# Turning the second sequence's first norm on VectorE and by transfers, with one feature order for both sequences and the mask made earlier

## The chip, the core and the metric

One core of one Trainium2 chip runs the whole program. Its engines, as the profile names them, are PE (TensorE: matmuls and transposes, with PEld for the loading of its weights), DVE (VectorE), ACT (ScalarE), POOL (GpSimd) and SP (SyncE, which issues most of the transfers). They run beside each other and wait for each other at semaphores. The metric is the device time of one execution in microseconds (us), as a median over runs. All arithmetic is in 32-bit floats.

## The reference

Two sequences of 512 tokens with 256 features go through four sublayers, each of the form `x = x + layernorm(f(layernorm(x)))`:

```python
x = x + _layernorm(_L0_attn_ref(_layernorm(x), ...))   # 16 heads of 128, causal
x = x + _layernorm(_L0_ffn_ref(_layernorm(x), ...))    # 4-bit weights, 2048 hidden
x = x + _layernorm(_L1_attn_ref(_layernorm(x), ...))   # linear attention
x = x + _layernorm(_L1_ffn_ref(_layernorm(x), ...))    # 16-entry table, 688 hidden
```

The change lies in the first line. The attention begins with a second norm, which has a gain and an offset for each feature, and then makes q, k and v:

```python
x = (h - mu) * rsqrt(var + EPS) * ln_g + ln_b
q = (x @ wq.T + bq); k = (x @ wk.T + bk); v = (x @ wv.T + bv)
q, k = rope(q), rope(k)
attn = softmax(where(causal, -inf, q @ k.T * scale))
```

## The kernel before, in words

**Tiles.** A sequence is four tiles of 128 tokens (`NT`), a token's 256 features are two chunks of 128 (`NK`). The norm is made with tokens on the partitions (tile `n`), but the projections contract over the features, so the normed values must be turned: `xT0[b]` holds, for sequence b, the features on the partitions and the 512 tokens along them. `xTv[b]` is a copy of it with the tokens in another order, for v. For both sequences, PE turned the tiles before (`turn`, L622, which calls `transpose`, L277), into a PSUM bank; `affine` (L625) then applied gain and offset on the way from the bank to `xT0`.

**first_norms (L564)** does this. It is a generator: at each `yield` it hands back the time until it wants to go on. For sequence 0 (`wait` is 0, L646 on) it works as fast as it can, because nothing else can start before: tiles 0 and 1 are centred by ACT (L657) and turned and scaled by a matmul with a diagonal; tiles 2 and 3 are centred by DVE (`centred`, L611) and turned by PE. For sequence 1 (L631 on) it makes one tile's statistics at a time (`statistics`, `variance`, `factor`, `finished`) and then, chunk by chunk, four transposes into a bank and one `affine`. At the end both copy `xT0` to `xTv` (L696), and later make the residual for their attention (L705 on).

**Later norms** (`norms`, L342) turn in the other way already: DVE transposes the tile in blocks of 32 by 32 into `tr` (L375), and four transfers (L379) bring the blocks to their partitions. The features then lie in another order along the partitions, and the weights that are contracted with them are laid out to fit on the host (`turned`, L1395). `chunk` (L319) reads such a tile in runs of 32.

**The order of the work.** Heads of both sequences are 32 slots (`slot`, L1021). In slot i, PE makes the scores of head i, the projections of head i+1, the output projection of head i-2, the attention of head i-1 and a part of v. DVE adds the mask and finds the minima (`scores`), ACT takes exponentials, DVE, ACT and POOL apply the rotation to q and k (`projection`, L802). POOL adds the two parts of k as its last step in a slot, and the scores of the next slot need this k. Only for head 0 does DVE add k (L846). Beside this, the 4-bit weights are dequantised in steps put off by `behind`, and the table weights are built by `look_up`, a DVE and a POOL instruction a step.

The order is fixed when the program is built. A planner adds up assumed costs (`Engine.cost`, L109) into a clock `now`, and `poll` (L250) lets every chain go on by a step whose due time has come. In a slot, `poll` is called twice near the end (L1112 and L1119), with a part of v between. `begin(first_norms(1, 6.0), 60.0)` (L1142) gives sequence 1's norm its start, 60 planned us after the first head's preparation, and 6 planned us between steps. Each engine's instructions, and SP's transfers, then run in the order in which they were written.

**The mask** is a tile of 128 by 512: cleared by POOL at the start (L560), and its causal part is filled by one `affine_select` on POOL (L1130). That stood after the two projections of head 0, and ahead of the first v and of head 1's q.

Of the kernel before, what the change touches and what calls it, by code (L numbers as in the profile page):

```python
# [10 lines left out]
F32 = mybir.dt.float32  # L11
# [8 lines left out]
P = 128  # L20
B = 2
# [167 lines left out]
def sandwich_kernel(  # L189
# [309 lines left out]
    with ExitStack() as at:  # L499
# [49 lines left out]


        xTv = [ac.tile([P, NK, S], F32, name=f"xTv_{b}") for b in range(B)]
        xT0 = [ac.tile([P, NK, S], F32, name=f"xT0_{b}") for b in range(B)]
        acc = ac.tile([P, NT, D], F32, name="h")


# [8 lines left out]
        def first_norms(b, wait):  # L564

            n = [
                acts.tile([P, HT, D], F32, tag="ln", name=f"n0_{b}_{j}") for j in range(NT // HT)  # L570
            ]
            st = small.tile([P, NT, 6], F32, tag="st0", name="st0", bufs=2)
            mv = small.tile([P, NT, 2], F32, tag="mv0", name="mv0", bufs=2)
            ve = small.tile([P, 2, NT], F32, tag="ve0", name="ve0", bufs=2)
            rstd = small.tile([P, 2, NT], F32, tag="rstd0", name="rstd0", bufs=2)
            shift = small.tile([P, 2, NT], F32, tag="shift0", name="shift0", bufs=2)

            def factors(k, ts, scale, more):
                vector.tensor_scalar(
                    ve[:, k, ts], mv[:, ts, 1], scale, more, ALU.mult, ALU.add  # L580
                )
                pool.tensor_tensor(rstd[:, k, ts], ve[:, k, ts], mhalf[:, ts], ALU.pow)

            def shifted(k, ts):
                vector.scalar_tensor_tensor(
                    shift[:, k, ts], mv[:, ts, 0], -1.0, rstd[:, k, ts], ALU.mult, ALU.mult
                )

            def norm(k, t, to):
                scalar.activation(  # L590
                    to,
                    x0[b][:, t, :],
                    AF.Identity,
                    bias=shift[:, k, t : t + 1],
                    scale=rstd[:, k, t : t + 1],
                )

            def finished(t):
                shifted(0, slice(t, t + 1))
                norm(0, t, n[t // HT][:, t % HT, :])  # L600

            def statistics(t):
                vector.bn_stats(st[:, t, :], x0[b][:, t, :])

            def variance(t):
                vector.bn_aggr(mv[:, t, :], st[:, t, :])

            def factor(t):
                factors(0, slice(t, t + 1), 1.0 + EPS, EPS * EPS)

            def centred(t):  # L611

                vector.tensor_scalar(
                    n[t // HT][:, t % HT, :],
                    x0[b][:, t, :],
                    mv[:, t, 0:1],
                    rstd[:, 0, t : t + 1],
                    ALU.subtract,
                    ALU.mult,
                )  # L620

            def turn(pt, kc, t):  # L622
                transpose(pt, n[t // HT][:, t % HT, kc * P : (kc + 1) * P])

            def affine(engine, to, pt, kc):  # L625
                if engine is scalar:
                    scalar.activation(to, pt, AF.Identity, bias=col("b", kc), scale=col("g", kc))
                else:
                    vector.tensor_scalar(to, pt, col("g", kc), col("b", kc), ALU.mult, ALU.add)

            if wait:  # L631
                for t in range(NT):
                    statistics(t)
                    variance(t)
                    factor(t)
                    if t:
                        finished(t - 1)
                    yield wait
                finished(NT - 1)
                yield 2 * wait  # L640
                for kc in range(NK):
                    pt = bank("t")
                    for t in range(NT):
                        turn(pt[:, t * P : (t + 1) * P], kc, t)
                    affine(scalar, xT0[b][:, kc, :], pt, kc)
                    yield wait  # L646
            else:

                minus = wu[:, 0, :P]
                scalar.mul(minus, ident, -1.0)
                for t in range(NT):
                    statistics(t)
                    variance(t)
                    if t < HT:
                        scalar.activation(  # L657
                            n[0][:, t, :], x0[b][:, t, :], AF.Identity, bias=mv[:, t, 0:1], scale=-1.0
                        )
                    factor(t)  # L660
                    if t < HT:
                        scalar.activation(
                            wu[:, 0, (t + 1) * P : (t + 2) * P],
                            minus,
                            AF.Identity,
                            scale=rstd[:, 0, t : t + 1],
                        )

                quarters = [[bank(tag) for _ in range(NK)] for tag in "ts"]
                for t in range(HT):  # L670
                    for kc in range(NK):
                        matmul(
                            quarters[0][kc][:, t * P : (t + 1) * P],
                            n[0][:, t, kc * P : (kc + 1) * P],
                            wu[:, 0, (t + 1) * P : (t + 2) * P],
                            True,
                            True,
                        )
                    if t == 0:
                        warm_up(2)  # L680
                centred(2)
                centred(3)
                for j in range(2):
                    if j:
                        yield 0.0
                        for kc in range(NK):
                            for t in (HT, HT + 1):
                                turn(quarters[1][kc][:, t % HT * P : (t % HT + 1) * P], kc, t)
                    for kc in range(NK):
                        affine(  # L690
                            scalar,
                            xT0[b][:, kc, j * TU : (j + 1) * TU],
                            quarters[j][kc][:, :TU],
                            kc,
                        )
            for kc in range(NK):  # L696
                (scalar.copy if kc or wait else pool.tensor_copy)(
                    xTv[b][:, kc, :].rearrange("p (t a j) -> p t j a", t=NT, j=4),
                    xT0[b][:, kc, :].rearrange("p (t j a) -> p t j a", t=NT, j=4),
                )  # L700
            yield 30.0
            while holder[0] is not None:
                yield 4.0
            holder[0] = b
            every = slice(0, NT)  # L705
            factors(1, every, 1.0, EPS)
            yield 2.0
            shifted(1, every)
            yield 2.0
            for t in range(NT):  # L710
                norm(1, t, acc[:, t, :])
                pool.tensor_add(acc[:, t, :], acc[:, t, :], bo_sb)
                yield 3.0

        first = first_norms(0, 0.0)
        next(first)

        def dequantised(packed, scales, u, name, w):

# [82 lines left out]
        def projection(kind, i, tag="mm"):  # L802
# [10 lines left out]
            for cs in [slice(0, TU), slice(TU, S)] if i == 0 else [slice(0, S)]:  # L813
                ps = bank(tag)
                for kc in range(NK):
                    matmul(
                        ps[:, cs],
                        w[:, hh, kc, :],
                        xT0[b][:, kc, cs],
                        kc == 0,  # L820
                        kc == NK - 1,
                    )
# [304 lines left out]
        next(pair[1])  # L1127
        for step in (*pair, *pair):
            next(step, None)
        pool.affine_select(  # L1130
            out=mask,
            in_=mask,
            compare_op=ALU.is_ge,
            fill=NEG,
            base=S - P,
            pattern=[[-1, S]],
            channel_multiplier=1,
        )
        values(0, 0, "t")
        project("q", 1, "o")  # L1140

        begin(first_norms(1, 6.0), 60.0)  # L1142
        main = ffn_hidden(0)
        for i in range(NS + 2):
            slot(i)
# [227 lines left out]
def _layout(i):  # L1373
# [4 lines left out]
    a0, f0, a1, f1 = "L0_attn_", "L0_ffn_", "L1_attn_", "L1_ffn_"  # L1378

    def by_group(w):  # L1380
        return w.reshape(NG, HG * DK, NK, P).transpose(0, 3, 2, 1)

    def by_head_chunk(w):
        return w.reshape(NG, HG, DK, NK, P).transpose(0, 4, 1, 3, 2)

    def by_head(v):
        return v.reshape(-1, P).T
# [10 lines left out]
    def by_half(s):  # L1398
# [16 lines left out]
        "wk": by_head_chunk(i[a0 + "wk"]),  # L1415
        "wv": by_group(i[a0 + "wv"]),
        "wo": i[a0 + "wo"].reshape(D, NG, HG, DK).transpose(1, 3, 2, 0),
        "cols": np.concatenate([by_head(i[a0 + n]) for n in ("bq", "bk", "bv", "ln_g", "ln_b")], axis=1),
        "bo": i[a0 + "bo"][None, :],
        "cos": np.concatenate([cos, cos]),  # L1420

# [33 lines left out]
```

## Time and profile before

| what | us |
|---|---|
| median of 3 runs | 628.33 |
| lowest and highest run | 627.58, 628.52 |
| the profiled execution's own time | 627.55 |
| its span, first to last instruction | 625.8 |
| PE busy in it | 618.7 |
| DVE busy | 486.7 |
| ACT busy | 299.4 |
| POOL busy | 277.6 |

The profile comes from one execution, and durations taken from it add up to its span, not to the median of the runs. A row of the timeline gives start and duration; several like instructions that follow each other are one row with a count. Matmuls overlap in PE, so that the distance from start to start, not the duration, says what one costs. Slots can be recognised by the rows `ps_s<-kT,qT` on PE: slot 0 starts at 15.16, slot 5 at 65.69 and slot 10 at 121.71. The last scores of the 32 slots are masked at about 362 us; what follows is mostly the three other sublayers.

### The profile page before, as it was taken

To read this page: it belongs to the slowest core of one execution; us is meant where nothing else is said; L and a number is where in the kernel's file an instruction comes from. 1 tells how busy PE (TensorE), PEld (TensorE's weight loads), DVE (VectorE), ACT (ScalarE), POOL (GpSimd) and SP (SyncE) were. 2 spreads that over 40 slices of the span, in tenths; PEclk is the share of its full clock that TensorE was granted. 3 is DMA by queue.
4 is the path that set the end of the run, shared out by engine and by line. 5 is a ranking of instruction groups with operands and counts; after the bars stand their busy time and mean duration, and the time that the engine had idled before them with its cause. 6 is when DMAs were issued, how large, how long until landed. Compare 5 with 4: busy or idle time off the path is not lost.

```text
span 625.8 us, 8236 instructions
## 1 busy us (share of the span) xinstructions
PE 618.7 (99%) x2512; PEld 462.7 (74%) x2512; DVE 486.7 (78%) x1155; ACT 299.4 (48%) x659; POOL 277.6 (44%) x350
## 2 busy tenths in 40 slices
PE   8999999999999999999999999999999999999996
PEld 6666666666666666666666778888888888888886
DVE  6879789877887989999988988869986373284853
ACT  5656666656655556656556661232313404416130
POOL 5264657455454375675667400350261151163341
PEclk9999999999999999999999999999999999999999
DMA  7467374564656646556453422211001001001000
GB/s 252 108 158 213 96 201 128 125 174 123 139 158 143 170 126 167 153 133 181 119 139 77 89 57 62 101 35 34 1 5 30 1 1 35 0 1 34 26 26 18
DMA packets 43004, 60.07 MB, mean 96 GB/s; under 512 B 5072, under 2 KB 30928, under 8 KB 42960
## 3 DMA queue, kind: packets, MB, share of 16 engines
q1 hardware_dynamic: 42672, 59.39, 36.5%
q8 instruction: 20, 0.33, 0.2%
q14 instruction: 24, 0.20, 0.1%
q10 hardware_dynamic: 288, 0.16, 0.1%
HBM read 28.33 MB, written 1.05 MB: 47 GB/s over the span
## 4 chain that ended last, share of the span: by engine, by line
PE 97%; DMA 1%; POOL 1%; ACT 0%; issue 0%; DVE 0%; SPq 0%; POOLq 0%
PE ps_mm L272 39%; PE ps_s L272 22%; PE ps_o L272 21%; PE ps_t L272 14%; DMA x<-in_x 0%; DMA cos_sb<-in_cos 0%; ACT xT L181 0%; PE ps_t L278 0%; POOL qT L181 0%; ACT xTv L181 0%; POOL ra L181 0%; DVE kT L181 0%; SPq L163 0%; POOLq L1451 0%; POOL rstd L181 0%
## 5 line engine op out<-in xcount | busy, mean ns | idle before, releaser
L181 DVE SCALAR_TENSOR_TENSOR rr<-ps_mm,cols_sb,sin_sb 64x512 f32<-64x512 f32 (+1 forms) x126 | 93.4, 741 | 3.8 <-PE ps_mm L272 1.0
L181 POOL TENSOR_TENSOR wg<-wg,scratch 128x752 f32<-128x752 f32 x30 | 53.6, 1787 | 92.0 <-DVE scratch L181 89.2
L272 PE MATMUL ps_mm<-xT,wg 128*128 128x256 f32 (+1 forms) x352 | 84.9, 379 | 0.0
L181 ACT ACTIVATE p<-p,mn 128x512 f32<-128x512 f32 (+3 forms) x128 | 70.6, 553 | 29.4 <-DVE mn L181 29.4
L272 PE MATMUL ps_s<-xT,wu 128*128 128x256 f32 x336 | 81.0, 379 | 0.0
L272 PE MATMUL ps_o<-wd,hT 128*128 128x256 f32 (+1 forms) x364 | 78.2, 372 | 0.0
L272 PE MATMUL ps_t<-pT,v 128*128 128x512 f32 (+3 forms) x256 | 74.2, 433 | 0.0
L272 PEld LDWEIGHTS ps_o<-wd,hT 128*128 128x128 f32 x364 | 67.4, 190 | 8.8
L272 PEld LDWEIGHTS ps_mm<-xT,wg 128*128 128x128 f32 (+1 forms) x352 | 66.4, 189 | 9.3 <-ACT ge L181 0.3
L272 PEld LDWEIGHTS ps_s<-xT,wu 128*128 128x128 f32 x336 | 63.8, 190 | 8.8
L272 PEld LDWEIGHTS ps_t<-pT,v 128*128 128x128 f32 x256 | 48.6, 190 | 27.9 <-issue 16.3
L181 DVE CUSTOM_DVE_ANT_0 p<-ps_s,mask 128x512 f32<-128x512 f32 (+2 forms) x96 | 45.8, 509 | 28.4 <-PE ps_s L272 28.2
L181 ACT ACTIVATE p<-p,rs 128x512 f32<-128x512 f32 (+3 forms) x128 | 61.4, 550 | 10.7 <-DVE rs L181 8.8
L272 PEld LDWEIGHTS ps_o<-wo,oT 128*128 128x128 f32 x256 | 48.6, 190 | 19.0 <-issue 12.9
L181 POOL TENSOR_TENSOR qT<-ra,rr 128x512 f32<-128x512 f32 x32 | 40.8, 1276 | 48.8 <-DVE rr L181 48.8
L272 PE MATMUL ps_s<-kT,qT 128*128 128x512 f32 (+2 forms) x192 | 60.8, 452 | 0.2 <-DVE kT L181 0.2
L272 PE MATMUL ps_o<-wo,oT 128*128 128x256 f32 x256 | 60.5, 379 | 0.0
L272 PE MATMUL ps_mm<-xT,wq 128*128 128x512 f32 (+1 forms) x128 | 58.6, 580 | 0.4 <-ACT xT L181 0.4
L272 PE MATMUL ps_mm<-xT,wk 128*128 128x512 f32 x124 | 58.3, 592 | 0.0
L272 PEld LDWEIGHTS ps_s<-kT,qT 128*128 128x128 f32 x192 | 36.0, 190 | 26.9 <-issue 15.0
L181 DVE STREAM_TRANSPOSE turned<-p 128x512 f32<-128x512 f32 (+3 forms) x128 | 54.1, 480 | 1.6 <-ACT p L181 0.7
L272 PE MATMUL ps_mm<-wv,xTv 128*128 128x256 f32 x232 | 54.9, 379 | 0.0
(146 smaller groups left out, 914.9 us busy)
## 6 DMA issues: line engine op xcount, KB each, us to landing
pT<-turned SPq DMA_DIRECT2D x128, 208.0 KB, 3.9
wo<-in_wo SPq DMA_DIRECT2D x17, 256.0 KB, 4.0
wv<-in_wv SPq DMA_DIRECT2D x16, 256.0 KB, 4.1
wq<-in_wq SPq DMA_DIRECT2D x15, 256.0 KB, 4.0
wk<-in_wk SPq DMA_DIRECT2D x15, 256.0 KB, 4.0
xT<-tr SPq DMA_DIRECT2D x44, 64.0 KB, 2.2
pk_g<-in_gate_p SPq DMA_DIRECT2D x4, 256.0 KB, 5.2
sc_g<-in_gate_s SPq DMA_DIRECT2D x8, 128.0 KB, 4.7
```

Of the source, the lines that this page charges most:

```text
L181: return write(*args, **more)
L272: nc.tensor.matmul(out, lhsT=lhsT, rhs=rhs, start=start, stop=stop, **more)
```

## The change

- The turning of sequence 1 leaves PE. Its four tiles are transposed by DVE in blocks of 32 by 32 into a part of `wd` (a tile that is filled later), and four transfers of 32 partitions each bring the blocks into `xT0[1]`, which gets the shape of a turned tile. `affine` then works on `xT0[1]` in place, from SBUF to SBUF, and the projections of sequence 1 read it through `chunk`.
- The feature order that results holds for both sequences, since they share the weights. For sequence 0, the two statements that write `n` (the DVE one in `centred` and the ACT one) read their tile through a view (`spread`), so that PE's transposes come out in this order; reading goes in steps of 32 floats, writing is in a row.
- The weights and the two columns for gain and offset are laid out to fit on the host.
- The mask's select is issued on POOL right after the first part of sequence 0's norm, ahead of the projections.
- Sequence 1's norm is due after 45 planned us instead of 60, with waits of 1 instead of 6.

The diff:

```diff
--- before.py
+++ after.py
@@ -549,7 +549,11 @@
 
 
         xTv = [ac.tile([P, NK, S], F32, name=f"xTv_{b}") for b in range(B)]
-        xT0 = [ac.tile([P, NK, S], F32, name=f"xT0_{b}") for b in range(B)]
+
+
+        xT0 = [
+            ac.tile([P, NK, S] if b == 0 else [P, 4, NK, NT, 32], F32, name=f"xT0_{b}") for b in range(B)
+        ]
         acc = ac.tile([P, NT, D], F32, name="h")
 
 
@@ -608,11 +612,19 @@
             def factor(t):
                 factors(0, slice(t, t + 1), 1.0 + EPS, EPS * EPS)
 
+            def spread(t):
+
+                return (
+                    n[t // HT][:, t % HT, :].rearrange("p (k f c) -> p k f c", k=NK, c=4),
+                    x0[b][:, t, :].rearrange("p (k c f) -> p k f c", k=NK, c=4),
+                )
+
             def centred(t):
 
+                to, x = spread(t)
                 vector.tensor_scalar(
-                    n[t // HT][:, t % HT, :],
-                    x0[b][:, t, :],
+                    to,
+                    x,
                     mv[:, t, 0:1],
                     rstd[:, 0, t : t + 1],
                     ALU.subtract,
@@ -637,12 +649,26 @@
                         finished(t - 1)
                     yield wait
                 finished(NT - 1)
-                yield 2 * wait
+                yield until(*n)
+
+                tr = wd.rearrange("p o d -> p (o d)")[:, : NK * S].rearrange(
+                    "p (c k j t) -> p c k j t", c=4, k=NK, j=NT
+                )
+                for t in range(NT):
+                    vector.transpose(
+                        tr[:, :, :, t, :],
+                        n[t // HT][:, t % HT, :].rearrange("p (k c f) -> p c k f", k=NK, c=4),
+                    )
+                    yield wait
+                for a in range(4):
+                    sync.dma_start(
+                        out=xT0[b][:, a].rearrange("p k j t -> p (k j t)"),
+                        in_=tr[32 * a : 32 * a + 32].rearrange("f c k j t -> f c (k j t)"),
+                    )
+                yield until(xT0[b])
                 for kc in range(NK):
-                    pt = bank("t")
-                    for t in range(NT):
-                        turn(pt[:, t * P : (t + 1) * P], kc, t)
-                    affine(scalar, xT0[b][:, kc, :], pt, kc)
+                    x = xT0[b][:, :, kc].rearrange("p a j t -> p a (j t)")
+                    affine(scalar, x, x, kc)
                     yield wait
             else:
 
@@ -655,7 +681,7 @@
                     variance(t)
                     if t < HT:
                         scalar.activation(
-                            n[0][:, t, :], x0[b][:, t, :], AF.Identity, bias=mv[:, t, 0:1], scale=-1.0
+                            *spread(t), AF.Identity, bias=mv[:, t, 0:1], scale=-1.0
                         )
                     factor(t)
                     if t < HT:
@@ -696,7 +722,9 @@
             for kc in range(NK):
                 (scalar.copy if kc or wait else pool.tensor_copy)(
                     xTv[b][:, kc, :].rearrange("p (t a j) -> p t j a", t=NT, j=4),
-                    xT0[b][:, kc, :].rearrange("p (t j a) -> p t j a", t=NT, j=4),
+                    xT0[b][:, kc, :].rearrange("p (t j a) -> p t j a", t=NT, j=4)
+                    if b == 0
+                    else xT0[b][:, :, kc].rearrange("p j t a -> p t j a"),
                 )
             yield 30.0
             while holder[0] is not None:
@@ -714,6 +742,15 @@
 
         first = first_norms(0, 0.0)
         next(first)
+        pool.affine_select(
+            out=mask,
+            in_=mask,
+            compare_op=ALU.is_ge,
+            fill=NEG,
+            base=S - P,
+            pattern=[[-1, S]],
+            channel_multiplier=1,
+        )
 
         def dequantised(packed, scales, u, name, w):
 
@@ -816,7 +853,7 @@
                     matmul(
                         ps[:, cs],
                         w[:, hh, kc, :],
-                        xT0[b][:, kc, cs],
+                        chunk(xT0[b], kc) if b else xT0[b][:, kc, cs],
                         kc == 0,
                         kc == NK - 1,
                     )
@@ -1127,19 +1164,10 @@
         next(pair[1])
         for step in (*pair, *pair):
             next(step, None)
-        pool.affine_select(
-            out=mask,
-            in_=mask,
-            compare_op=ALU.is_ge,
-            fill=NEG,
-            base=S - P,
-            pattern=[[-1, S]],
-            channel_multiplier=1,
-        )
         values(0, 0, "t")
         project("q", 1, "o")
 
-        begin(first_norms(1, 6.0), 60.0)
+        begin(first_norms(1, 1.0), 45.0)
         main = ffn_hidden(0)
         for i in range(NS + 2):
             slot(i)
@@ -1378,10 +1406,10 @@
     a0, f0, a1, f1 = "L0_attn_", "L0_ffn_", "L1_attn_", "L1_ffn_"
 
     def by_group(w):
-        return w.reshape(NG, HG * DK, NK, P).transpose(0, 3, 2, 1)
+        return w.reshape(NG, HG * DK, NK, 4, 32).transpose(0, 4, 3, 2, 1).reshape(NG, P, NK, HG * DK)
 
     def by_head_chunk(w):
-        return w.reshape(NG, HG, DK, NK, P).transpose(0, 4, 1, 3, 2)
+        return w.reshape(NG, HG, DK, NK, 4, 32).transpose(0, 5, 4, 1, 3, 2).reshape(NG, P, HG, NK, DK)
 
     def by_head(v):
         return v.reshape(-1, P).T
@@ -1415,7 +1443,11 @@
         "wk": by_head_chunk(i[a0 + "wk"]),
         "wv": by_group(i[a0 + "wv"]),
         "wo": i[a0 + "wo"].reshape(D, NG, HG, DK).transpose(1, 3, 2, 0),
-        "cols": np.concatenate([by_head(i[a0 + n]) for n in ("bq", "bk", "bv", "ln_g", "ln_b")], axis=1),
+        "cols": np.concatenate(
+            [by_head(i[a0 + n]) for n in ("bq", "bk", "bv")]
+            + [turned(by_head(i[a0 + n])) for n in ("ln_g", "ln_b")],
+            axis=1,
+        ),
         "bo": i[a0 + "bo"][None, :],
         "cos": np.concatenate([cos, cos]),
```

## The prediction

> **What bounds the kernel now.** I read four views: the head of the page, what TensorE (PE) waited for, the timeline where the changed lines run, and the timeline of the first 23 us. The columns of a timeline are start, duration (us), engine, line, operation, tiles, shapes, count and the idle time before.
>
> ```profile
> span 625.8 us, 8236 instructions
> PE 618.7 (99%) x2512; PEld 462.7 (74%) x2512; DVE 486.7 (78%) x1155; ACT 299.4 (48%) x659; POOL 277.6 (44%) x350
> PE 97%; DMA 1%; POOL 1%; ACT 0%; issue 0%; DVE 0%; SPq 0%; POOLq 0%
> ```
>
> PE is the chain that ends last. Its waits in the whole execution are four, and all lie in the first 16 us:
>
> ```profile
> PE ps_o L546 <- POOL ident masks.py:199: 1.4, 1, 1.4
> PE ps_mm L272 <- ACT xT L181: 0.4, 1, 0.4
> PE ps_t L272 <- ACT wu L181: 0.3, 1, 0.3
> PE ps_s L272 <- DVE kT L181: 0.2, 1, 0.2
> ```
>
> So time can come from PE work that is removed, or from the start. VectorE (DVE), busy 78%, is next, but nothing in PE waits for it later. The work removed, at its first place, with its neighbours:
>
> ```profile
> 131.18 1.89 PE L272 MATMUL ps_mm<-wv,xTv 128*128 128x256 f32 x8
> ...
> 132.91 0.60 PE L278 MATMUL ps_t<-ident,n 128*128 128x128 f32 x4
> ...
> 133.35 1.89 PE L272 MATMUL ps_s<-kT,qT 128*128 128x512 f32 x6
> ```
>
> Four transposes stand between the starts 132.91 and 133.35, so they cost 0.44 us, not the 0.60 of the row and not four times their 0.272. The slots confirm it: the scores start at 99.30, 110.50 and 121.71 (11.2 us apart) and then at 133.35 and 144.99 (11.64 apart, in both cases with four transposes inside).
>
> At the start, the mask and what stands around it:
>
> ```profile
> 12.64 1.27 POOL L181 TENSOR_TENSOR qT<-ra,rr 128x512 f32<-128x512 f32 x1
> 13.08 1.88 PE L272 MATMUL ps_o<-xT,wq 128*128 128x512 f32 x4
> ...
> 13.86 0.61 POOL L181 TENSOR_SCALAR_AFFINE_SELECT mask<-mask 128x512 f32<-128x512 f32 x1
> 13.94 1.08 DVE L181 TENSOR_TENSOR kT<-ra,rr 128x512 f32<-128x512 f32 x1
> ...
> 15.16 1.96 PE L272 MATMUL ps_s<-kT,qT 128*128 128x512 f32 x6 [0.20 <-DVE kT L181]
> ...
> 21.72 0.66 DVE L181 TENSOR_TENSOR kT<-ra,rr 128x512 f32<-128x512 f32 x1
> ```
>
> The same addition takes 1.08 us beside the mask's select and 0.66 alone. The first scores wait for its end at 15.02.
>
> [...] The trace has this pair already (tr<-ln at 0.426 us for 128x256; xT<-tr landing in 2.2 us).
>
> **The change, part by part.**
>
> PE work removed: eight transposes in two groups of 0.44 make **-0.88**. Nothing follows them that hides it, as PE waits for nothing there. The projections of the second sequence now read xT0 in runs of 32. I take zero: ps_t<-pT,v reads runs of 32 and has 592 ns for 512 columns, wq from plain xT0 also 592; 256 columns from xT1 in runs have 379, as from plain weights. A gain is excluded, since nothing there is shortened; were each of the 128 matmuls (0.43 us) 1% longer, it would be 0.5, which I keep as the upper bound.
>
> VectorE added: four transposes of 0.426, 1.7 us, over two slots of 11.2 us. ScalarE: the affine reads SBUF, not PSUM; the same size from SBUF is 0.72 (p<-p,rs) against 0.78, so nothing. The two xTv copies (2.04 us together) stay at one place.
>
> The start of the norm moves from 60 to 45 planned us and its waits from 6 to 1. The planner polls twice near the end of a slot, some 1.7 us apart, and before the first statistics ran at 75.9, the end of slot 5 (slot 5 starts at 65.69). Fifteen us earlier is the end of slot 4, and now both polls serve it: tiles 0 and 1 at the end of slot 4, tiles 2 and 3 at the end of slot 5, the last shift in slot 6, transposes in slots 6 to 8, transfers then, affines and copies in slots 9 to 11. xTv is first read at the end of slot 14 and xT0 in slot 15 (from 178.6): over 30 us of cover, and without it every late us would stop PE.
>
> A tile step is 0.79 us on VectorE (75.91 to 76.70), 0.87 with a shift. Slot 4 gains 1.7 us: VectorE waited 2.43 us at 66.75 for PE, which hides it. Slot 5 has two steps in place of one, +1.0 us: there VectorE is already late, its scores start at 78.35 where PE's are ready at about 77.5. Of the 1.0, 0.45 is taken up by its wait ahead of ra at 81.04. The other 0.55 reaches POOL's last step for the slot:
>
> ```profile
> 83.47 1.28 POOL L181 TENSOR_TENSOR qT<-ra,rr 128x512 f32<-128x512 f32 x1 [1.02 <-DVE rr L181]
> 84.69 1.28 POOL L181 TENSOR_TENSOR ra<-ra,cos_sb 128x512 f32<-128x512 f32 x1
> 86.06 1.28 POOL L181 TENSOR_TENSOR kT<-ra,rr 128x512 f32<-128x512 f32 x1
> ```
>
> kT ends at 87.34 and PE wants it at 88.10, so 0.76 is free and 0.2 is left: **0**, bounds 0 and +0.6. In slots 6 to 9 two transposes (0.85) replace one step (0.87): 0. Each shift now waits, within a slot, for POOL's power (0.55 us, 1.54 [...]); behind it on VectorE stand the dequantised weights' product (1.41) and the next scores, for which ScalarE's exponentials and then kT wait. That is the 0.6.
>
> SyncE (SP): four transfers of 128 KB go into its queue, some 2.9 to 3.3 us of issue as for xT<-tr and pT, behind the pT transfers of that slot and ahead of the next slot's loads. They wait for the four transposes. Behind them stand weights for two slots later, whose loads take 4 us: 0. If that cover were gone, 3 us would be PE's.
>
> The mask: its select goes behind the four powers on POOL, the last of which ends at 7.13, where POOL was idle until 9.37. kT then takes 0.66 and ends at 14.60. Now PE's own queue is late next: 13.08 and four matmuls of 0.43 give 14.80 against 15.16, so **-0.36** at most.
>
> What it meets there: centred(3) on VectorE starts at 7.16, waiting for the same power, and is a tensor_scalar from SBUF. POOL goes first. The earlier centred(2), 0.14 longer (below), holds the fourth power to about 7.27; the select ends near 7.88 [...]; centred(3) ends at about 8.33. Its transpose was due at 8.25 (8.11 and 0.14), so PE is late by about 0.13.
>
> The feature order: both statements write in a row and read in steps of 32. ScalarE has the form at 599.87:
>
> ```profile
> 599.87 0.83 ACT L181 ACTIVATE ln<-x,shift,rstd 128x256 f32<-128x256 f32 x1 [2.05 <-POOL shift L181]
> ```
>
> 0.83 against 0.60 for the plain one: +0.23. The first such instruction ends at 4.74 instead of 4.51, hidden by the wait for the power (wu starts at 4.84). The second delays wu from 5.97 to 6.20, and PE's matmuls, which followed the warm-up at 6.18, to about 6.25: +0.07. On VectorE, [...] I take 0.14 (0.41 becomes 0.55)[...]. The 0.07 and 0.13 fall on one path and don't add: **+0.14**, bounds 0.05 and 0.5. It could not be below zero, since nothing there is shortened.
>
> Sum: -0.88 - 0.36 + 0.14 = -1.10. The profiled execution has 627.55 (span 625.8 and 1.75 around it), so 626.45. The median of the runs, 628.33, lies 0.78 above it; with the same step, **627.2**.
>
> **Rivals.** (1) The start gives nothing: select and hops delay PE by the whole 0.36 or by up to 0.3 more. For it: transpose and centred(3) are only 0.1 us apart. Against: PE needs this only once. 627.45 to 627.8. (2) The start gives all, and the earlier scores free VectorE too: 628.33 - 0.88 - 0.36 = 627.1, down to 626.6. [...] (3) Slower: two tile steps a slot put the POOL powers onto VectorE's path. If each waits the 1.54 of the row at 77.30, VectorE is 2.1 us late; 0.45 and 0.76 absorb 1.2, so 0.9 us a slot reaches PE through kT; in four slots 3.6, that is 628.33 - 1.1 + 3.6 = 630.8. It decides from 1.2 us of lateness, and to be slower outright takes 2.4 us in all. Against: in slot 5 the power stands ahead of the product that would block it. (4) The order written out after slot 16 comes out otherwise, because the planner's clock stands 0.9 us lower: either sign, about 1 us.
>
> **Numbers.** Chances: the sum as it stands (626.8 to 627.5) 0.45, rival 1 0.20, rival 2 0.15, rival 3 0.12, rival 4 0.08. 0.2% of 628.33 is 1.26 us, about what this measurement tells from no change; the sum lies just inside. Faster by more: 0.4 of the first case, rival 2 and a third of rival 4, 0.38; slower: rival 3, 0.12; between: 0.50. The range, 626.5 to 628.7, leaves out rival 3 and the edges.
>
> **What would show it.** PE's x8 group from n at 272 ns gone and slots 10 and 11 at 11.2 us; kT's first at 0.66; first scores near 14.94; n<-x,mv near 0.73 on ScalarE and 0.55 on VectorE; no PE wait for kT at slot 7. Wrong would be: slots 4 to 9 longer than 11.2, or projections above 592 ns.

## The result and the profile after

| | before | after |
|---|---|---|
| median of 22 runs each, taken side by side (us) | 628.11 | 626.80 |
| lowest and highest | 627.49, 628.66 | 626.49, 627.73 |
| the profiled execution's own time | 627.55 | 626.75 |
| its span | 625.8 | 625.0 |

The ratio is 0.9983, with a 95% interval from 0.9976 to 0.9989: about 1.1 us faster (0.7 to 1.5), where 1.1 was forecast. The means of the runs lie 1.09 us apart, the medians 1.31. The interval leaves out 1, so it is a gain, though at 0.17% it lies inside the 0.2% that the prediction took as the limit of what can be told from no change.

The head of the page and its chain of work, by engine:

```profile
span 625.0 us, 8231 instructions
PE 618.0 (99%) x2504; PEld 462.0 (74%) x2504; DVE 488.3 (78%) x1159; ACT 299.9 (48%) x659; POOL 276.7 (44%) x350
PE 98%; DMA 0%; issue 0%; DVE 0%; POOL 0%; ACT 0%; POOLq 0%
```

PE has eight instructions less, VectorE four more. What PE's matmuls waited for in the whole execution:

```profile
PE ps_o L546 <- POOL ident masks.py:199: 1.4, 1, 1.4
PE ps_mm L272 <- ACT xT L181: 0.4, 1, 0.4
PE ps_t L272 <- ACT wu L181: 0.3, 1, 0.3
```

In this list the wait for kT is gone and no other has come. (The loads of PE's weights have a list of their own. It has one wait of 0.2 us for POOL's kT before and two after; what the new one costs is told below, after the terms of the sum.) The slots that held the transposes, on PE's timeline:

```profile
121.53 1.89 PE L272 MATMUL ps_s<-kT,qT 128*128 128x512 f32 x6
132.73 1.89 PE L272 MATMUL ps_s<-kT,qT 128*128 128x512 f32 x6
143.93 1.89 PE L272 MATMUL ps_s<-kT,qT 128*128 128x512 f32 x6
```

They are 11.20 us apart, where before they were 11.64: twice 0.44. The start:

```profile
6.43 0.53 DVE L181 TENSOR_SCALAR n<-x,mv,rstd 128x256 f32<-128x256 f32 x1
...
7.34 0.61 POOL L181 TENSOR_SCALAR_AFFINE_SELECT mask<-mask 128x512 f32<-128x512 f32 x1
7.41 0.78 DVE L181 TENSOR_SCALAR n<-x,mv,rstd 128x256 f32<-128x256 f32 x1 [0.45 <-POOL rstd L181]
...
8.49 0.60 PE L278 MATMUL ps_s<-ident,n 128*128 128x128 f32 x4
...
14.10 0.69 DVE L181 TENSOR_TENSOR kT<-ra,rr 128x512 f32<-128x512 f32 x1
14.96 1.94 PE L272 MATMUL ps_s<-kT,qT 128*128 128x512 f32 x6
```

The first kT takes 0.69 us, not 1.08, and PE's scores follow its own queue. The centred tile beside the select takes 0.78 us where the one before it takes 0.53, so now it is this tile that takes longer beside the select, but it ends at 8.19, ahead of the group of transposes that begins at 8.49, of which its own is the second: nothing waits for it.

**Reading differences below 1 us.** The two traces don't begin alike: the first tokens landed 0.13 us later in the second (first statistics at 3.46, not 3.33). So I compare distances between two events of one trace. From the first statistics (`st<-x` on VectorE) to the first projection (`ps_mm<-xT,wq`) it was 4.00 us before and 4.04 after: this holds what the feature order costs. From there to the first scores it was 7.83 before (7.33 to 15.16) and 7.46 after (7.50 to 14.96): the mask. The sum of the three is -0.88 - 0.37 + 0.04 = -1.21. By the scores of slot 12 the trace after is 1.06 us ahead, and 1.19 if the later landing is set aside. Not all of it lasts: of the two spans, less what lies ahead of the first statistics, 622.4 and 621.5 us are left, 0.9 apart.

### The profile page after: what moved, and what is told of

Read it like the earlier page. It is cut to its first block, busy times and chain, and to the rows that moved or that the text cites. A ratio compares the mean times of both kernels' runs of the same rounds, so it can differ in the third digit from the quotient of the medians.

```text
span 625.0 us, 8231 instructions
## 1 busy us (share of the span) xinstructions
PE 618.0 (99%) x2504; PEld 462.0 (74%) x2504; DVE 488.3 (78%) x1159; ACT 299.9 (48%) x659; POOL 276.7 (44%) x350
## 3 DMA queue, kind: packets, MB, share of 16 engines
HBM read 28.33 MB, written 1.05 MB: 47 GB/s over the span
## 4 chain that ended last, share of the span: by engine, by line
PE 98%; DMA 0%; issue 0%; DVE 0%; POOL 0%; ACT 0%; POOLq 0%
PE ps_mm L272 39%; PE ps_o L272 22%; PE ps_s L272 22%; PE ps_t L272 15%; DMA x<-in_x 0%; POOL rstd L181 0%; DVE st L181 0%; POOLq L1483 0%; ACT xT L181 0%; DVE x L181 0%; PE ps_o L546 0%; PE ps_s L278 0%; PE ps_t L278 0%; ACT wu L181 0%; DVE mv L181 0%
```

## The experiments

**Theory:** PE's time is the kernel's; the change takes 0.88 us from PE and 0.37 from one wait at the start, and everything that it adds is hidden. **Rivals:** the select costs the start in its new place what it gives (prediction, rival 1); the earlier start of the norm, or another order of the work, carries the gain (rival 4 in kind); and VectorE and POOL have no room for the added steps (rival 3). All ratios are to the kernel before, with 95% intervals. It was timed again beside each group of kernels, and its median was 627.78 beside e1 to e4, 627.74 beside e5 to e8 and 627.79 beside e9 to e11; the 628.11 of the table stood beside the changed kernel. So kernels of different groups are compared by their ratios, not by their medians.

| kernel | statistics to projection | projection to scores | slots that are not 11.2 | median us | ratio |
|---|---|---|---|---|---|
| before | 4.00 | 7.83 | 11.64, 11.64 | 628.11 | |
| after | 4.04 | 7.46 | none | 626.80 | 0.9983 (0.9976 to 0.9989) |
| e1 mask back | 4.47 | 7.83 | none | 627.31 | 0.9989 (0.9983 to 0.9996) |
| e2 mask only | 4.00 | 7.46 | 11.64, 11.64 | 627.48 | 0.9994 (0.9986 to 1.0002) |
| e3 order only | 4.03 | 7.80 | 11.64, 11.64 | 628.02 | 1.0003 (0.9995 to 1.0011) |
| e4 PE turns again | 4.95 | 7.46 | 12.08 | 627.99 | 0.9999 (0.9991 to 1.0007) |
| e5 turned twice | 4.87 | 7.82 | 12.08, 12.08 | 628.60 | 1.0016 (1.0010 to 1.0023) |
| e6 select twice | 4.20 | 7.46 | none | 626.85 | 0.9984 (0.9978 to 0.9991) |
| e7 mask first | 4.57 | 7.47 | none | 627.26 | 0.9991 (0.9983 to 0.9999) |
| e8 burst | 4.03 | 7.46 | 13.09, 11.31 | 628.85 | 1.0018 (1.0011 to 1.0024) |
| e9 start at 60 | 4.14 | 7.47 | none | 626.88 | 0.9987 (0.9980 to 0.9993) |
| e10 warm-up early | 4.51 | 7.47 | none | 626.83 | 0.9982 (0.9975 to 0.9988) |
| e11 no warm-up | 5.11 | 8.37 | none | 628.37 | 1.0008 (1.0002 to 1.0015) |

The fourth column is over slots 4 to 20. The first four slots together agree within 0.05 us with those of the kernel before, except in e2, e3 and e5, where they are 0.14, 0.18 and 0.07 longer; I did not follow why. After 245 us a few slots have 0.05 to 0.1 more, and the last ones differ in kind; both are left out. The second column scatters for a reason of its own, which e10 and e11 take up.

**e1: the select back at its old place, in the changed kernel.**

```diff
         next(first)
-        pool.affine_select(out=mask, ...)
...
+        pool.affine_select(out=mask, ...)
         values(0, 0, "t")
```

> The changed kernel with the mask's select at its old place on POOL. Theory (the select beside kT cost PE 0.36 us at the start, the rest of the change at the start costs 0.04): the first kT takes 1.08 us again, from the first statistics to the first scores it is 11.83 to 11.9 us (11.50 in the changed kernel, 11.83 in the one before), all slots stay at 11.2 us, and the time lies about 0.35 us above the changed kernel, 0.9 below the one before. Rival (the select in its new place costs as much as it gives): no difference from the changed kernel, 11.5 us.

The timeline at the first kT of this kernel:

```profile
14.41 0.61 POOL L181 TENSOR_SCALAR_AFFINE_SELECT mask<-mask 128x512 f32<-128x512 f32 x1
14.50 1.07 DVE L181 TENSOR_TENSOR kT<-ra,rr 128x512 f32<-128x512 f32 x1
```

kT is long again, and 7.83 us lie between projection and scores. The expected 11.83 to 11.9 from the statistics came out as 12.30, because PE took 1.18 us for the first group, where it took 0.71 in the changed kernel (4.47 in the second column; see e10); the select stands far behind that group here, at 14.41. By the ratios (0.9989 and 0.9983) the mask is worth 0.4 us, but the intervals overlap; the traces say 0.37.

**e2: the select ahead, alone, in the kernel before.** The same lines are moved in the other direction.

> The kernel before with only the select moved ahead. Theory: kT takes 0.66 us, first statistics to first scores 11.47 us, slots 10 and 11 stay at 11.64, and the time is about 0.36 us below before. Rival ([...]): 11.6 us and 0.2 below before, or nothing.

```profile
7.05 0.61 POOL L181 TENSOR_SCALAR_AFFINE_SELECT mask<-mask 128x512 f32<-128x512 f32 x1
7.12 0.69 DVE L181 TENSOR_SCALAR n<-x,mv,rstd 128x256 f32<-128x256 f32 x1 [0.44 <-POOL rstd L181]
```

From projection to scores it was 7.46 us, and 4.00 ahead of that as in the kernel before: rival 1's 0.13 isn't there. The centred tile took 0.69 us, not 0.41, and yet PE did not wait for it. The median moved by 0.3 us against the kernel before beside it, and the interval includes no change, so the runs alone don't show this gain. The trace shows 0.37 at the first scores, of which the longer first slots of this kernel leave 0.23.

**e3: the feature order alone**, with both sequences turned by PE and all else as before.

```diff
-                norm(0, t, n[t // HT][:, t % HT, :])
+                to, x = spread(t)
+                scalar.activation(to, x, AF.Identity,
+                    bias=shift[:, 0, t : t + 1], scale=rstd[:, 0, t : t + 1])
```

and the views, weights and columns of the change.

> The kernel before with only the feature order of the change: both sequences are written through the view with steps of 32 floats, both are turned by PE as before, the select stands at its old place, the norm starts after 60 planned us. Theory (after the trace of the changed kernel): ACT's instruction 0.73 and VectorE's 0.53 us, yet only 0.04 us at the first scores (11.87 us from the first statistics), so the time is that of before within what can be measured. Rival (my prediction's 0.14): 11.97 us and 0.14 above before. For the four ACT instructions of sequence 1 0.83 in place of 0.60 us each, hidden.

4.03 against 4.00: up to the first projection the order costs 0.03 us, and nothing at the first scores (11.83 in both, where kT came last), though ACT's instruction takes 0.74 and VectorE's 0.53. The same 4.03 and 4.04 stand in e8 and in the changed kernel.

**e4: PE turns sequence 1 again, in the changed kernel.** The eight transposes and the affine from PSUM return, with the plain shape of `xT0[1]` and the reads that go with it; the feature order stays.

```diff
-                for t in range(NT):
-                    vector.transpose(...)
-                    yield wait
-                for a in range(4):
-                    sync.dma_start(...)
-                yield until(xT0[b])
                 for kc in range(NK):
-                    x = xT0[b][:, :, kc].rearrange("p a j t -> p a (j t)")
-                    affine(scalar, x, x, kc)
+                    pt = bank("t")
+                    for t in range(NT):
+                        turn(pt[:, t * P : (t + 1) * P], kc, t)
+                    affine(scalar, xT0[b][:, kc, :], pt, kc)
```

> The changed kernel with sequence 1 turned by PE again (in the new feature order, eight transposes, the affine from PSUM); mask, start at 45 planned us and waits of 1 stay. Theory (PE work alone decides): two slots, or one, are longer by 0.44 us a group, 0.88 in all, and the time is 0.88 above the changed kernel, about 0.2 to 0.4 below before. Rival (the relief of the PSUM bank or a changed order elsewhere is part of the gain): the loss differs from 0.88 by more than 0.2, and other slots change too.

```profile
88.85 1.89 PE L272 MATMUL ps_s<-kT,qT 128*128 128x512 f32 x6
...
98.33 0.60 PE L278 MATMUL ps_t<-ident,n 128*128 128x128 f32 x4
...
100.49 0.60 PE L278 MATMUL ps_t<-ident,n 128*128 128x128 f32 x4
100.93 1.89 PE L272 MATMUL ps_s<-kT,qT 128*128 128x512 f32 x6
```

Both groups fell into one slot, from 88.85 to 100.93, which is 12.08 us long: 0.88 more. No other slot changed. So in the slots nothing but PE's own work was in this part of the gain. By the ratios the loss is 1.0 us (0.9999 against 0.9983).

**e5: the eight transposes issued twice, in the kernel before.**

```diff
-                    for t in range(NT):
+                    for t in (*range(NT), *range(NT)):
                         turn(pt[:, t * P : (t + 1) * P], kc, t)
```

> The kernel before, with each of sequence 1's eight transposes issued twice on PE, into the same bank. Theory: 0.88 us more than before, slots 10 and 11 at 12.08 us. Rival (PE has slack that hides small work): no difference from before.

PE's scores and the doubled groups between them:

```profile
122.59 1.89 PE L272 MATMUL ps_s<-kT,qT 128*128 128x512 f32 x6
...
133.79 1.04 PE L278 MATMUL ps_t<-ident,n 128*128 128x128 f32 x8
134.67 1.89 PE L272 MATMUL ps_s<-kT,qT 128*128 128x512 f32 x6
```

133.79 to 134.67 is 0.88 for eight, 0.11 for each. Both slots are 12.08 and the time is 0.16% up (0.10 to 0.23). With e4 this settles the price from both sides.

**e6: two selects in the new place.**

```diff
         pool.affine_select(out=mask, in_=mask, ...)
+        pool.affine_select(out=mask, in_=mask, ...)
```

> The changed kernel with the mask's select issued twice in its new place, which gives the same mask. Theory: in the changed kernel the second centred tile ends 0.2 us before its transpose is due; [...] PE's transposes come about 0.4 late and so do the first scores: 11.9 us from the first statistics, 0.4 us above the changed kernel. Rival (the cover there is larger, or the select does not hold VectorE up): no difference.

```profile
7.16 1.33 POOL L181 TENSOR_SCALAR_AFFINE_SELECT mask<-mask 128x512 f32<-128x512 f32 x2
7.23 0.77 DVE L181 TENSOR_SCALAR n<-x,mv,rstd 128x256 f32<-128x256 f32 x1 [0.45 <-POOL rstd L181]
```

The expectation failed. The two selects span 7.16 to 8.49, 1.33 us where one alone takes 0.61, and yet the centred tile takes 0.77 us, as with one (0.78), and ends at 8.00, 0.49 us ahead of them.

**e7: the select right behind the clearing of the mask**, at 1.87 us, where POOL has nothing to do.

```diff
         pool.memset(mask, 0.0)
+        pool.affine_select(out=mask, in_=mask, ...)
```

> The changed kernel with the select right behind the clearing of the mask, where POOL waits for the first statistics. Theory (the centred tile is not on the path): the second centred tile takes 0.53 us in place of 0.78, and nothing else moves: 11.50 us to the first scores, the time of the changed kernel. Rival ([...]): 11.37 us and 0.13 below the changed kernel.

```profile
7.24 0.50 DVE L181 TENSOR_SCALAR n<-x,mv,rstd 128x256 f32<-128x256 f32 x1 [0.45 <-POOL rstd L181]
```

The centred tile fell from 0.78 to 0.50, and projection to scores stayed (7.47). It is the cleaner place, but no gain: the ratio (0.9991) lies above the changed kernel's (0.9983) and the intervals overlap. In the trace the difference is in the second column (4.57, not 4.04): PE's first group took 1.22 us, not 0.71.

**e8: all four tile steps at once, at the end of slot 5.**

```diff
                     if t:
                         finished(t - 1)
-                    yield wait
...
-        begin(first_norms(1, 1.0), 45.0)
+        begin(first_norms(1, 1.0), 60.0)
```

> The changed kernel with all four tile steps of sequence 1's norm in one go at the end of slot 5 (start after 60 planned us), in place of two at the end of slot 4 and two at the end of slot 5. Theory (POOL's kT has 0.85 us left and VectorE about 0.1 in slot 6): VectorE comes 1.5 us later to the scores of slot 6 than in the changed kernel (about 80.0), kT for slot 7 comes 0.5 to 0.6 too late, and the time is 0.5 us or more above the changed kernel. Rival (the cover is larger): slots stay at 11.2 us and the time is the changed kernel's.

The longest of PE's waits, and the timeline that leads to it:

```profile
PE ps_s L272 <- POOL kT L181: 1.7, 1, 1.7
```

```profile
77.33 0.16 DVE L181 SCALAR_TENSOR_TENSOR shift<-mv,rstd 128x1 f32<-128x1 f32 x1 [0.45 <-POOL rstd L181]
...
79.70 0.16 DVE L181 SCALAR_TENSOR_TENSOR shift<-mv,rstd 128x1 f32<-128x1 f32 x1 [0.60 <-POOL rstd L181]
...
80.92 0.68 DVE L181 CUSTOM_DVE_ANT_0 p<-ps_s,mask 128x512 f32<-128x512 f32 x1
...
88.10 1.27 POOL L181 TENSOR_TENSOR kT<-ra,rr 128x512 f32<-128x512 f32 x1
...
89.42 1.99 PE L272 MATMUL ps_s<-kT,qT 128*128 128x512 f32 x6 [1.72 <-POOL kT L181]
```

The same place in the changed kernel:

```profile
76.71 1.89 PE L272 MATMUL ps_s<-kT,qT 128*128 128x512 f32 x6
...
78.44 0.68 DVE L181 CUSTOM_DVE_ANT_0 p<-ps_s,mask 128x512 f32<-128x512 f32 x1
...
85.80 1.27 POOL L181 TENSOR_TENSOR kT<-ra,rr 128x512 f32<-128x512 f32 x1
...
87.92 1.89 PE L272 MATMUL ps_s<-kT,qT 128*128 128x512 f32 x6
```

VectorE came to the scores 4.59 us after PE had begun them (76.33), where in the changed kernel it came after 1.73: 2.86 later. The slot was 13.09 us, 1.89 longer. So 0.97 us were absorbed, which is what the changed kernel's own trace shows to be free (kT ends at 87.07, PE wants it at 87.92: 0.85; VectorE has 0.1 ahead of ra). The theory had the room right and the lateness too small, 1.5: two shifts waited 1.05 us in all for POOL's powers. This is rival 3's mechanism, a late VectorE that reaches PE through kT, made to happen. Since e9 below has the same start at 60 without the loss, it is the burst that does it. It shows that the change stays clear of it by how the steps are spread, not by its nature.

**e9: the start at 60 planned us, with the short waits.**

```diff
-        begin(first_norms(1, 1.0), 45.0)
+        begin(first_norms(1, 1.0), 60.0)
```

> The changed kernel with sequence 1's norm due after 60 planned us in place of 45, waits of 1 as in the change: everything of it comes one slot later. Theory (the earlier start is only there so that the longer way is done in time; the gain is PE's 0.88 and the mask's 0.36): all slots 11.2 us, 7.46 us from the first projection to the first scores, the time of the changed kernel. Rival (the start or its place in the slots carries part of the gain): slots 5 to 12 differ, the time by more than 0.4.

The slots and the start are those of the changed kernel, but for 0.10 us in the second column, where PE's first group took 0.86 us and not 0.71. The ratio, 0.9987 against 0.9983, tells no difference. The earlier start is no part of the gain.

**e10 and e11: the warm-up.** The changed kernel's PE, before its first real work, multiplies the identity by itself 8 times (`warm_up`). e10 lets it read a zeroed part of the mask's tile instead, and nine times; e11 leaves these eight out.

```diff
+    pool.memset(mask[:, :P], 0.0)
     pool.memset(mhalf, -0.5)
...
-WARM = 8
+WARM = 9
-    nc.tensor.matmul(warm[:, :P], lhsT=ident, rhs=ident, ...)
+    nc.tensor.matmul(warm[:, :P], lhsT=mask[:, :P], rhs=mask[:, :P], ...)
```

> The changed kernel with PE's warm-up matmuls reading a zeroed part of the mask's tile in place of the identity, so that they start some 0.4 us earlier, and nine of them in place of eight. Theory ([...] the first four matmuls of the diagonal took 0.71, 0.92, 1.18 or 1.22 us in the executions profiled, and the first projection starts 4.0 or up to 4.95 us after the first statistics): the slow case becomes rarer, so the median falls by up to 0.4 and the highest runs disappear. Rival ([...]): the same median and scatter as the changed kernel.

> The changed kernel without the first eight warm-up matmuls (the two in between stay). Theory: [...] the first group takes 1.22 us, the first projection starts 5 us or more after the first statistics, and the time is 1 to 3 us above the changed kernel; from the first scores on nothing differs. Rival (PE's speed at the start is not what scatters): no difference.

e10 began its warm-up at 0.98 us in place of 1.38, and its first group still took 1.22 us. The ratio is the changed kernel's (0.9982 and 0.9983); the highest run is 0.4 lower (627.32), but over 21 runs, beside another group, that shows little. That an earlier warm-up makes the long first group rarer is not shown. By the ratios e11 was 1.6 us above the changed kernel. Its first group took 1.22 us, and its first four matmuls of the projections (`ps_mm<-xT,wq`, 128x256) 2.06 where they took 1.16 in the changed kernel, so that it was 8.37 us from projection to scores. The warm-up was worth those 1.6 us here. The one trace of an earlier beginning, e10's, shows PE no faster in the first group.

## Why the prediction was right, step by step

- **PE's transposes, -0.88:** exact, by the slots (twice 0.44), by e4 (+0.88) and e5 (+0.88). Reading them from start to start (0.44 us for four), not from their durations (0.60), was the step that mattered.
- **The mask, -0.36:** 0.36 or 0.37 in every pair of traces, wherever the select stands away from kT (e1, e2, e6, e7). That PE's own queue would be next was right: 13.24 and four times 0.43 is 14.96.
- **The start's cost, +0.14:** too large; 0.04. The ACT term (+0.07) measured 0.03. The VectorE term (0.13) measured nothing: the centred tile ended at 8.19, not 8.33, and its transpose, the second of the group at 8.49, came well after it. The price of reading in steps was about right (0.41 became 0.53); the 0.55 that was forecast was an estimate of mine, which no trace of before showed for VectorE. What failed is that one and the same stretch was counted too long: the forecast had 1.06 us from the select's start (7.27) to the tile's end (8.33), while the pair measured 0.85 (7.34 to 8.19). It let the tile's 0.55 begin at 7.78, when most of the select would be over, and that was an estimate too. The tile lost only 0.25 us of the 0.54 for which the select ran beside it (before, kT lost 0.42 of 0.53). Why the two lost differently is open.
- **Slot 5's lateness, +1.0, of which 0.55 was to reach POOL's last step:** it was +0.27 (scores 1.73 us after PE's, 1.46 before). The second step filled 0.32 us in which VectorE had been idle, and the product behind it took 1.22, not 1.41. kT had 0.85 left, not 0.2. The zero in the sum stands, and e8 shows where it would end.
- **POOL's powers:** the wait came, behind the two tile steps at the end of slot 4, where a shift stood 0.91 us for a power (at 66.50) in time that VectorE had free.
- **SP's four transfers, 0:** issued in 2.94 us from 124.02, behind pT and ahead of the next weights, as forecast; landed in 3.1 to 4.0 us; nobody waited.
- **VectorE's four transposes:** cheaper than forecast, two in 0.73 us. ACT's affine from SBUF took 0.80, not 0.72, also hidden. The projections from runs of 32 kept 592 ns.
- **The later order (rival 4):** the instructions after slot 16 stand in the same order on every engine in both traces, so it didn't happen.

The sum was -1.10, and the runs give -1.1 (-0.7 to -1.5). The three places add up to -1.21 in the traces, and about -0.9 is left at the end. The mechanism was right, but that the number agrees so well is in part luck: the prediction took 0.10 us too much at the start, and put two later losses, 0.25 together, at nothing. The absolute 627.2 came out as 626.80; 0.2 of that is the kernel before, which had 628.11 here and not the 628.33 of its three first runs. (The chances that the prediction names add up to 0.36 for faster by more and 0.52 for between, not to 0.38 and 0.50.)

**The two later losses.** One is slot 24, which is 11.29 us long and was 11.20. POOL's last step and PE's scores there, after and before:

```profile
277.09 1.27 POOL L181 TENSOR_TENSOR kT<-ra,rr 128x512 f32<-128x512 f32 x1
...
278.44 1.97 PE L272 MATMUL ps_s<-kT,qT 128*128 128x512 f32 x6
```

```profile
277.98 1.28 POOL L181 TENSOR_TENSOR kT<-ra,rr 128x512 f32<-128x512 f32 x1
...
279.50 1.89 PE L272 MATMUL ps_s<-kT,qT 128*128 128x512 f32 x6
```

kT now ends 0.08 us ahead of the scores, where it ended 0.24 ahead. The load of PE's weights waited 0.22 us for it, and the row of scores takes 1.97 us in place of 1.89: 0.08 of the lead are gone. So in this slot too kT is what PE waits for when VectorE and POOL come late. Longer slots, this one or the one ahead of it, stand in e1, e4, e7, e9 and e11 too and not in e2, e3, e5, e6, e8 and e10; why VectorE and POOL were later in some kernels I did not follow.

The other loss is the end. From the start of PE's last matmul to the end of the span it is 5.01 or 5.02 us in the five kernels in which PE turns sequence 1 (before, e2, e3, e4, e5), and 5.18 to 5.20 in the changed kernel, e1, e6, e7 and e8, in which VectorE and the transfers do. In the two traces of before and after it is SP's last wait, for the result to land, that differs, 1.2 us and then 1.4. After and before:

```profile
SPq L1483 <- DMA out<-x: 1.4, 1, 1.4
SPq L1451 <- DMA out<-x: 1.2, 1, 1.2
```

As e4 has all else of the change and 5.02 us, the turning without PE gives back 0.17 us there of its 0.88. What made the last transfer land later is open.

No kernel tried is faster than the changed one by more than the intervals.

## What to carry to other kernels

Where one engine is the chain and waits for nothing, an operation taken from it was worth its distance from start to start here (0.44 us for four transposes), and that could be read before anything was changed. The work moved to other engines was free only up to the room between their last product in a stage and the moment when the bound engine wants it: find that pair of rows (here POOL's kT and PE's scores, 0.85 us apart) and spread the added steps so that none exceeds it. For differences under 1 us in a kernel of 600, measure between two events inside each trace, since the start scatters by as much (4.00 to 4.95 us from statistics to projection with the warm-up in place); then follow the lead to the last instruction, since part of it can be lost again.

## What the runs showed of the hardware that I had not expected

**PE's speed at the start.** The same four matmuls of the first group took 0.71 us in five kernels (before, after, e2, e3, e8) and 0.86 to 1.22 in the others, with the same code on PE up to that point except in e10 and e11. The timeline of e4, where it came latest with the warm-up in place:

```profile
5.46 1.22 PE L272 MATMUL ps_t<-wu,n 128*128 128x128 f32 x4 [0.30 <-ACT wu L181]
6.47 1.06 PE L546 MATMUL ps_o<-ident 128*128 128x128 f32 x4
7.33 0.67 PE L272 MATMUL ps_t<-wu,n 128*128 128x128 f32 x4
```

The next matmuls of the identity take 1.06 there and 0.61 in the changed kernel's trace. That moves the whole rest by up to 0.9 us (second column). It is of the size of the spread of a kernel's own runs (626.5 to 627.7 for the changed one), but with one trace for each kernel it isn't shown to be its cause. The clock granted to PE reads 1.00 in every stretch of the first 12 us, in e4 as in the changed kernel, so it doesn't tell the two apart. e10, whose warm-up began 0.40 us earlier, took 1.22 us for the group as well. What makes it slow is open.

**VectorE beside POOL's select.** The second centred tile took 0.78 us with one select beside it and 0.77 with two in POOL's queue (e6), where it took 0.50 with none (e7). kT took 1.08 us beside the select (before) and 0.69 without it (after).

**Reading in steps of 32 floats** added 0.23 to 0.24 us to ACT's instruction of 128x256 (0.51 and 0.49 before, 0.74 and 0.73 after) and 0.09 to 0.12 to VectorE's (0.41 before, 0.53 after and 0.50 in e7, where no select stands beside it).
